# A scan layer's product with C moved one group back, and the next layer's weights loaded into dead tiles

## The chip, the core and the metric

The kernel runs on one core of a Trainium2 chip. The core has five engines that matter here, each with its own instruction stream in program order: PE (TensorE, matrix products), DVE (VectorE), ACT (ScalarE), POOL (GpSimd) and SP, which issues the transfers (DMA). [...] The metric is the device time of one execution in microseconds (us).

## What is computed

Two layers on an image tensor `x` of shape (4, 384, 64, 64), both with a residual and a group norm ahead of them. Layer 0 is a selective scan (Mamba) over the 4096 pixels of each image, with 768 channels and 16 states per channel. Layer 1 is attention over 7 x 7 windows with 12 heads.

```python
# layer 0, per image (L = 4096 tokens, 768 channels, 16 states)
xz = einsum('blc,dc->bld', layernorm(xs), in_proj_w); xb, z = split(xz, 2)
xc = silu(causal_conv4(xb) + conv_b)
dt, Bm, Cm = split(einsum('bld,ed->ble', xc, x_proj_w))      # 24, 16, 16
dt = softplus(einsum('blr,dr->bld', dt, dt_w) + dt_b)
h  = exp(dt * A) * h + (dt * xc) * B         # the recurrence, over tokens
y  = sum_n(h * C) + xc * D
x  = x + einsum('bld,cd->blc', y * silu(z), out_proj_w)
# layer 1
qkv = w_qkv @ group_norm(x) + b_qkv
logits = q . k in the 7 x 7 window (edge padding) + rel_bias
x  = x + w_proj @ (softmax(logits) @ v window) + b_proj
```

## The kernel before

Layer 0 goes through 64 steps (4 images of 16 chunks of T = 256 tokens). A step has 24 groups `m`: a group is 4 of the 16 states of one block of 128 channels (6 blocks d). Each group is two half-groups, so that a step has 48 slots. The lists in `AT` say in which slot the other work is issued; negative slots lie in the step before.

A group passes through four engines. ACT makes the decays exp(dt A) in PSUM (two instructions for each half). DVE or POOL makes the drive `db` = (dt x) B. DVE scans, two states at a time. POOL multiplies by C, in place. PE transposes and adds up over the states.

```python
def driven(I, m, h, eng):                                      # DVE or POOL
    db = w2.tile([P, NG, T], F32, tag="db", bufs=6)
    dtx = dtx_ps[:, d % 2, :] if eng is nc.vector else h["dtx"][d]
    eng.tensor_tensor(db[:, :, 1:], <dtx over 4 states>, h["B"][g][:, :, 1:], ALU.mult)

def decay(I, m, half, k, h):                                   # ACT
    act(da_ps[half][:, k, 1:], h["dt"]..., AF.Exp, scale=nega[:, d, n : n + 1])

def scans(I, m, half, hs):                                     # DVE
    nc.vector.tensor_tensor_scan(hs[:, pair, :], da_ps[half], dbs[I, m][:, pair, :],
                                 0.0, ALU.mult, ALU.add)

def kept_states(I, m, hs):                                     # ACT
    nc.scalar.copy(state[:, d, g * NG : (g + 1) * NG], hs[:, :, T - 1])

def with_c(I, m, h, hs):                                       # POOL, in place
    nc.gpsimd.tensor_tensor(hs, hs, h["C"][m % (NS // NG)], ALU.mult)

def summed(I, m, h, hs):                                       # PE
    for k in range(NG):
        for half in range(2):
            nc.tensor.matmul(y[:, d % 2, half, :], hs[:, k, half * P : (half + 1) * P],
                             ident, is_transpose=True, ...)
```

`dtx` (POOL) is dt times xc, and `dtx_ps` ACT's copy of it in PSUM for DVE. When a pair p of channel blocks has been added up, it is turned: ACT copies `yt` to `ys`, PE turns it back and adds xc D, DVE multiplies by the gate `sz` into `yg` (four buffers). The slots are those of `AT["turn"]`. The output projection then reads all three `yg`.

The loop over the groups:

```python
behind = []
for n in range(STEPS * M):
    hs = w2.tile([P, NG, T], F32, tag="hs", bufs=5)
    for half in range(2):
        others, acts = plan[I][2 * m + half]
        if half == 0 and behind:
            acts.insert(0, lambda last=behind[-1]: kept_states(*last[:2], last[3]))
        if 2 * n + half + 1 < len(halves):
            acts.insert(0, <decay of the next half, k = 0>)
            acts.insert(2, <decay of the next half, k = 1>)
        for what in acts: what()
        if half == 0:
            if behind: with_c(*behind[-1])
            ready = len(behind) - 1
            ...                              # held back once at the start of a pair
            for _ in range(ready): summed(*behind.pop(0))
        scans(I, m, half, hs)
        for what in others: what()
    behind.append((I, m, steps[I], hs))
```

So in group n ACT is given the state copy of group n-1, POOL the product of n-1, and PE the sum of n-2.

Layer 1 begins with its weights and its first stripe of x:

```python
w_qkv = wt.tile([P, NJ, 3 * C], F32); nc.sync.dma_start(w_qkv, qkv_wT...)   # 1728 KB
w_pj  = wt.tile([P, NJ, C], F32);     nc.sync.dma_start(w_pj, proj_wT...)   #  576 KB
for m in range(NJ):
    for j in range(NJ):
        nc.tensor.matmul(pvb[:, m : m + 1], w_pj[:, j, ...], qkb[:, ...], ...)
nc.vector.tensor_tensor(pjb, pjb, pvb[:, :NJ], ALU.add)
...
def projected(b, s, h, pool=ps, tag="mm"):
    xr = w2.tile(...); xn = w2.tile(..., bufs=1)
    nc.sync.dma_start(xr, x1s[b][...])
    for j in range(NJ): nc.vector.tensor_scalar(xn[:, j], xr[:, j], <mean>, <1/std>, ...)
    ...                                      # products with w_qkv for k, v and q
```

## Time and profile before

The median of three runs is 8284.29 us (8283.61 to 8287.84); the profiled execution took 8284.12 us, with a mean granted clock of TensorE of 0.963. What the profile gives for the instructions that the change touches:

| group | engine | times | busy, us | mean of one, ns |
|---|---|---|---|---|
| product with C, `hs<-hs,C` (L669) | POOL | 1536 | 3622.9 | 2363 |
| drive `db<-dtx,B` (L637) | POOL | 512 | 1207.6 | 2359 |
| drive `db<-dtx_ps,B` (L637) | DVE | 1024 | 1223.1 | 1200 |
| scan `hs<-da,db` (L656) | DVE | 3072 | 3623.3 | 1211 |
| decay `da<-dt,nega` (L96) | ACT | 6144 | 2898.3 | 474 |
| transposing sum `y<-ident,hs` (L682) | PE | 12288 | 1667.1 | 283 |

A line of a profile names the line of the kernel (L669), the engine, the operation, output and inputs with their shapes and how often it ran. "Busy" is the time in which instructions of that group ran. "Idle before" is how long the engine stood still just ahead of them, and the name after an arrow is the instruction whose end let it go on. The granted clock is the share of TensorE's full clock that it was given. The chain of work that ended last is followed back from the last instruction: at each step to what released it, or to the instruction before it on its engine.

### The profile page before, as it was taken

How to read it: one execution, taken by the hardware profiler on the slowest of the kernel's cores; microseconds unless marked ns; L12 is line 12 of the kernel's file. 1: busy time of each engine (PE TensorE's matmuls, PEld its weight loads, DVE VectorE, ACT ScalarE, POOL GpSimd, SP SyncE). 2: the span in 40 equal slices, each digit the busy share in tenths (PEclk: the TensorE clock that was granted, in tenths of full speed). 3: DMA queues.
4: the chain of work that ended last, by engine and by line, in shares of the span. 5: the costliest groups of instructions: out<-in, count | busy, mean ns of one | idle time of the engine just before them, and what ended most of it. 6: DMA issues, size and time to landing. Idle time of an engine off the chain costs nothing.

```text
span 8282.4 us, 144249 instructions
## 1 busy us (share of the span) xinstructions
PE 7499.3 (91%) x48570; PEld 5769.9 (70%) x48570; DVE 6666.8 (80%) x9783; ACT 6079.0 (73%) x17509; POOL 6954.3 (84%) x5223
## 2 busy tenths in 40 slices
PE   6898998899998989898989899899799999999999
PEld 5777777777777777777777777777555555555555
DVE  5888888888888888888888888888666666666666
ACT  4888888888888888888888888888555455455455
POOL 3999998989999898999989899999677777677777
PEclk9999999999999999999999999999799999999999
DMA  3212211221222122212211211121222233222322
GB/s 96 77 60 66 77 59 55 66 72 58 65 74 65 55 59 73 64 61 72 68 53 59 66 61 55 60 71 51 79 85 86 85 89 88 81 88 81 87 85 64
DMA packets 459624, 583.93 MB, mean 71 GB/s; under 512 B 195036, under 2 KB 343276, under 8 KB 458756
## 3 DMA queue, kind: packets, MB, share of 16 engines
q1 hardware_dynamic: 458884, 574.69, 22.7%
q8 instruction: 387, 6.34, 0.3%
q14 instruction: 353, 2.89, 0.1%
HBM read 472.02 MB, written 84.73 MB: 67 GB/s over the span
## 4 chain that ended last, share of the span: by engine, by line
PE 44%; ACT 21%; POOL 17%; DVE 12%; issue 5%; DMA 0%; SPq 0%; POOLq 0%; DVEq 0%; ACTq 0%
POOL hs L669 11%; ACT da L96 8%; DVE hs L656 6%; PE mm_ps L419 6%; PE y L682 5%; PE pt_ps L1047 4%; PE mm_ps L574 4%; PE mm_ps L426 3%; PE lg_ps L1016 3%; POOL db L637 3%; PE mm_ps L920 3%; PE mm_ps L1100 3%; PE mm_ps L953 3%; PE mm_ps L983 3%; PE pv_ps L1073 3%
## 5 line engine op out<-in xcount | busy, mean ns | idle before, releaser
L669 POOL TENSOR_TENSOR hs<-hs,C 128x1024 f32<-128x1024 f32 x1536 | 3622.9, 2363 | 478.4 <-ACT state L665 421.2
L656 DVE TENSOR_TENSOR_SCAN hs<-da,db 128x512 f32<-128x512 f32 x3072 | 3623.3, 1211 | 357.8 <-ACT da L96 210.2
L96 ACT ACTIVATE da<-dt,nega 128x255 f32<-128x255 f32 x6144 | 2898.3, 474 | 699.3 <-DVE hs L656 670.8
L1037 POOL TENSOR_SCALAR sg<-sg,rsum 128x308 f32<-128x308 f32 x1536 | 1621.4, 1076 | 638.9 <-DVE rsum L1035 637.2
L682 PE MATMUL y<-ident,hs 128*128 128x128 f32 x12288 | 1667.1, 283 | 468.1 <-POOL hs L669 450.5
L682 PEld LDWEIGHTS y<-ident,hs 128*128 128x128 f32 x12288 | 1443.1, 146 | 728.2 <-POOL hs L669 590.9
L637 DVE TENSOR_TENSOR db<-dtx_ps,B 128x1020 f32<-128x1020 f32 x1024 | 1223.1, 1200 | 110.9 <-ACT dtx_ps L609 105.7
L637 POOL TENSOR_TENSOR db<-dtx,B 128x1020 f32<-128x1020 f32 x512 | 1207.6, 2359 | 1.4 <-DMA B<-bcrows 1.4
L419 PE MATMUL mm_ps<-xn,w_in 128*128 128x256 f32 x4608 | 1160.5, 400 | 1.9 <-DVE xn L390 1.9
L96 ACT ACTIVATE sg<-sg,mx 128x308 f32<-128x308 f32 x1536 | 828.8, 541 | 250.8 <-DVE mx L1022 221.8
L419 PEld LDWEIGHTS mm_ps<-xn,w_in 128*128 128x128 f32 x4608 | 919.6, 206 | 132.3 <-DVE xn L390 2.6
L1022 DVE CUSTOM_DVE_ANT_0 sg<-lg_ps,bias 128x308 f32<-128x308 f32 x1536 | 643.2, 475 | 382.1 <-PE lg_ps L1016 382.1
L426 PE MATMUL mm_ps<-xb,dcv 128*128 128x256 f32 x3072 | 772.7, 400 | 9.4 <-DVE gm_b L270 9.4
L1065 ACT COPY tb<-pt_ps 88x512 f32<-88x512 f32 x384 | 222.3, 579 | 625.5 <-PE pt_ps L1061 625.4
L426 PEld LDWEIGHTS mm_ps<-xb,dcv 128*128 128x128 f32 x3072 | 592.0, 199 | 112.5 <-issue 19.9
L729 PE MATMUL mm_ps<-yg,w_out 128*128 128x256 f32 x2304 | 551.4, 380 | 0.0
L1052 DVE COPY ta<-pt_ps 110x512 f32<-110x512 f32 x768 | 492.7, 683 | 23.3 <-PE pt_ps L1047 23.3
L729 PEld LDWEIGHTS mm_ps<-yg,w_out 128*128 128x128 f32 x2304 | 434.3, 191 | 57.0
L1047 PE MATMUL pt_ps<-ident,sg 128*110 128x128 f32 x3072 | 417.6, 279 | 0.9 <-POOL sg L1037 0.8
L1047 PEld LDWEIGHTS pt_ps<-ident,sg 128*110 128x110 f32 x3072 | 322.8, 133 | 78.0 <-issue 48.4
L920 PE MATMUL mm_ps<-xn,w_qkv 128*128 128x512 f32 (+2 forms) x612 | 277.7, 592 | 60.4 <-DVE xn L907 53.2
L1016 PE MATMUL lg_ps<-k,q 32*128 32x308 f32 x3072 | 311.3, 473 | 0.0
(154 smaller groups left out, 10400.7 us busy)
## 6 DMA issues: line engine op xcount, KB each, us to landing
B<-bcrows SPq DMA_DIRECT2D x256, 512.0 KB
C<-bcrows SPq DMA_DIRECT2D x256, 512.0 KB
vw<-vd SPq DMA_DIRECT2D x1792, 33.0 KB
xr<-x SPq DMA_DIRECT2D x28, 1056.0 KB
vd<-v SPq DMA_DIRECT2D x280, 96.0 KB
xi<-in_x_dram SPq DMA_DIRECT2D x64, 384.0 KB
xo<-in_x_dram SPq DMA_DIRECT2D x64, 384.0 KB
x<-xo SPq DMA_DIRECT2D x64, 384.0 KB
```

Of the source, the lines that this page charges most:

```text
L96: ins = nc.scalar.activation(o, i, func, **kw)
L419: nc.tensor.matmul(pb[:, k, :], w_in[:, j, m * P : (m + 1) * P], xn[:, j, :], start=(j == 0), stop=(j == NJ - 1),)
L426: nc.tensor.matmul(pb[:, k, :], dcv[:, d, c, :], xb[:, d, c : c + T], start=(c == 0), stop=(c == KC - 1),)
L637: eng.tensor_tensor(db[:, :, 1:], dtx[:, 1:].unsqueeze(1).broadcast_to([P, NG, T - 1]), h["B"][g][:, :, 1:], ALU.mult,)
L656: nc.vector.tensor_tensor_scan(hs[:, pair, :].rearrange("p k t -> p (k t)"), da_ps[half].rearrange("p k t -> p (k t)"), dbs[I, m][:, pair, ...
L669: nc.gpsimd.tensor_tensor(hs, hs, h["C"][m % (NS // NG)], ALU.mult)
L682: nc.tensor.matmul(y[:, d % 2, half, :], hs[:, k, half * P : (half + 1) * P], ident, is_transpose=True, start=(first and half == 0 and d % ...
L729: nc.tensor.matmul(po, w_out[:, d, m * P : (m + 1) * P], h["yg"][d // 2][:, d % 2, :], start=False, stop=(d == ND - 1),)
L1016: nc.tensor.matmul(lg[:, :NK], blk["q"][pr, m, bl, :, :].rearrange("p r c -> p (r c)"), blk["k"][pr, m, :, bl * CB : bl * CB + CW], start= ...
L1022: nc.vector.tensor_tensor_reduce(sg[:, hh, :], lg[:, :NK], bias[:, 4 * m + hh, :], -1.0, BIG, ALU.add, ALU.min, mx[:, hh : hh + 1],)
L1037: nc.gpsimd.tensor_scalar(sg[:, hh, :], sg[:, hh, :], rs[:, hh : hh + 1], None, ALU.mult)
L1047: nc.tensor.transpose(pt[: KN[c], col : col + P], sg[:, 2 * pair + hh, KOFF[c] : KOFF[c] + KN[c]], ident,)
```

## The change

Three things are changed in layer 0. POOL's product with C is given one group later: in group n it is that of n-2, and PE's sum that of n-3. For that `hs` gets six buffers instead of five. The aim is that POOL finds the scans done and the state copy made when it comes to a product. The state copy itself goes ahead of both decays of its slot. To make room, `ys` has one buffer instead of two and `yg` three instead of four. The slots in `AT` are set anew for this order.

At the seam, `w_in`, `dcv` and the tile `xo` are moved to a pool that lives through both layers. In the last step, `w_in` and `dcv` are no longer read, and layer 1's weights and first input are loaded into them. The first input is normalised there as well. The product of the projection with the value bias, which needs `w_pj`, moves behind the first stripe's projections.

```diff
-             'x': ((-11, -11, -8, -7), (-11, -11, -7, -5), (-7, -6, -4, -3)),
-             'c': ((-3, -2, 0, 5), (3, 3, 7, 8), (15, 16, 18, 19)),
+             'x': ((-11, -11, -8, -7), (-11, -11, -9, -6), (-7, -6, -4, -3)),
+             'c': ((-5, -4, -2, 1), (3, 3, 7, 8), (15, 16, 18, 19)),
 ... norm two slots later, single slots of z, burst and softplus changed by one or two
-             'dtx': (-5, -3, 9, 13, 23, 29),
+             'dtx': (-5, -4, 7, 12, 22, 28),
 ... driven: group 11 from DVE to POOL, group 16 from POOL to DVE, three slots changed
-             'turn': (21, 24, 26),
+             'turn': (23, 25, 28),
-             'e0': (-4, -2, 11, 12, 23, 26),
-             'h0': (-4, -1, 11, 16, 24, 32),
+             'e0': (-4, -2, 11, 13, 23, 23),
+             'h0': (-4, -1, 11, 16, 24, 35),
 ... two entries of first
@@ turn
-                    h["ys", p] = w2.tile([P, 2, 2, P], F32, tag="ys", ...)
+                    h["ys", p] = w2.tile([P, 2, 2, P], F32, tag="ys", ..., bufs=1)
-                    yg = w2.tile([P, 2, T], F32, tag="yg", ..., bufs=4)
+                    yg = w2.tile([P, 2, T], F32, tag="yg", ..., bufs=3)
@@ loads in the last step
+            def early():
+                nc.sync.dma_start(w_qkv, qkv_wT.rearrange("(k p) m -> p k m", p=P))
+                nc.sync.dma_start(w_pj, proj_wT.rearrange("(k p) m -> p k m", p=P))
+                nc.sync.dma_start(x_first..., x1s[0][:, : n0 * HW]...)
+            def early_normed():
+                for j in range(NJ):
+                    nc.vector.tensor_scalar(x_first[:, j, :, :], x_first[:, j, :, :],
+                        gms1[0][:, j, 0:1], gms1[0][:, j, 1:2], ALU.subtract, ALU.mult)
+            slot_of(STEPS - 1)(24, early)
+            slot_of(STEPS)(AT["turn"][2] - 15, early_normed)
@@ the loop over the groups
-                hs = w2.tile([P, NG, T], F32, tag="hs", ..., bufs=5)
+                hs = w2.tile([P, NG, T], F32, tag="hs", ..., bufs=6)
-                    if half == 0 and behind:
-                        acts.insert(0, lambda last=behind[-1]: kept_states(*last[:2], last[3]))
                     if 2 * n + half + 1 < len(halves):
                         ...
+                    if half == 0 and behind:
+                        acts.insert(0, lambda last=behind[-1]: kept_states(*last[:2], last[3]))
                     if half == 0:
-                        if behind:
-                            with_c(*behind[-1])
-                        ready = len(behind) - 1
+                        if len(behind) > 1:
+                            with_c(*behind[-2])
+                        ready = len(behind) - 2
-            with_c(*behind[-1])
+            for what in behind[-2:]:
+                with_c(*what)
@@ layer 1
-            w_qkv = wt.tile(...); nc.sync.dma_start(w_qkv, ...)
-            w_pj = wt.tile(...); nc.sync.dma_start(w_pj, ...)
-            ... product of w_pj with the value bias, here ahead of everything
+            def values_bias(): ...     # the same product
-            ahead = projected(*todo[0], stripes[0], ps_l, "lg")
+            ahead = projected(*todo[0], stripes[0], ps_l, "lg", xn=x_first)
             ...
             vw = window(*todo[0], 0)
+            values_bias()
```

## Prediction

> **What bounds the kernel now.** I read the busy shares first, then busy time by stage, the waits inside the first layer, the chain that ended last, and the seam between the layers. The page opens with busy time and share of each engine:

> ```profile
> PE 7499.3 (91%) x48570; PEld 5769.9 (70%) x48570; DVE 6666.8 (80%) x9783; ACT 6079.0 (73%) x17509; POOL 6954.3 (84%) x5223
> ```

> That average mixes two layers. By stage (columns: stretch in us, length, then PE, weight load, DVE, ACT, POOL busy with counts, granted clock, DMA share, GB/s):

> ```profile
> 3000.00:4000.00 1000.00, 900.44 (x4989) 760.11 (x4989) 891.51 (x857) 847.83 (x2402) 913.68 (x616) 0.96 0.21 66
> 7000.00:8282.00 1282.00, 1221.04 (x10958) 723.94 (x10955) 825.63 (x2667) 642.18 (x1995) 921.21 (x903) 0.99 0.28 82
> ```

> The first row is the scan layer (it ends at about 5954 us), the second the attention layer. In the scan layer four engines lie between 85% and 91%, so none is simply the bound, and each is idle for a tenth. From 1000 to 5700 us the trace has 1239 products with C; at 24 a step that is 51.6 steps, so a step takes 4700/51.6 = 91.0 us and a slot (48 a step) 1.90 us. The waits in that stretch (engine, line, waited for: us, times, longest):

> ```profile
> POOL hs L669 <- ACT state L665: 350.2, 401, 5.2
> ...
> ACT da L96 <- DVE hs L656: 538.3, 669, 6.0
> ...
> PE y L682 <- POOL hs L669: 339.0, 239, 2.8
> ...
> DVE yg L712 <- PE mm_ps L705: 163.7, 98, 2.6
> DVE db L637 <- ACT dtx_ps L609: 82.3, 101, 1.1
> ```

> POOL's only large wait is 350.2/51.6 = 6.8 us a step, for ACT's small copy of the last states: the product overwrites `hs` in place, so it must wait until ACT has read the last column, and ACT reaches that copy only after whatever stands before it. Does it matter? One stretch of the chain that ended last, in order of time (start, us, what):

> ```profile
> 4089.42 0.13 ACT state L665
> 4089.55 0.07 issue
> 4089.61 1.83 POOL hs L669
> 4091.44 0.49 issue
> 4091.93 0.73 POOL dtx L603
> 4092.66 2.21 POOL hs L669
> 4094.86 0.07 issue
> 4094.93 2.35 POOL db L637
> 4097.28 2.31 POOL hs L669
> 4099.60 0.04 issue
> 4099.64 1.97 PE y L682 x8
> 4101.61 5.89 PE mm_ps L419 x24
> ```

> ACT had been on the chain since 4059, with its burst of Silu and two table loads in it. Then the chain crosses to POOL by this very wait, stays 10 us there, and 14 us on PE, up to the gate on DVE at 4114.06. Counted over 1000 to 5700 us, it goes from ACT's state copy to POOL's product 124 times, 2.4 times a step. It spends 29% of that stretch on ACT, 27% on PE, 24% on POOL, 14% on DVE. So this wait is on the path, though not alone.

> The seam, PE's instructions with the idle time before them:

> ```profile
> 5951.49 2.75 PE L729 MATMUL mm_ps<-yg,w_out 128*128 128x256 f32 x12
> 5964.45 3.97 PE L879 MATMUL pvb<-qkb,w_pj 128*128 128x1 f32 x18 [10.20 <-DMA w_pj<-in_proj_wT_dram]
> 5969.53 12.83 PE L920 MATMUL lg_ps<-xn,w_qkv 128*128 128x192 f32 x36 [1.11 <-DVE xn L907]
> ```

> PE ends layer 0 at 5954.24 and starts attention's first projection at 5969.53: 15.3 us between, for the weights, the product with the bias and the first input.

> [...] here the two engines' drive products take 2359 and 1200 ns. POOL's work therefore can't be shrunk or cheaply moved, only its waiting. [...]

> **The change part by part.** *Product one group later.* At group n POOL now multiplies group n-2, whose scans and state copy were done about a group (3.8 us) ago. The waits of 0.87 us on average (350.2/401), 5.2 at most, should vanish nearly all. No instruction goes or comes: POOL's work stays 82.6 us a step (90.75% of 91.0). Removing all 6.8 us would be the upper bound. What the path gets back is less. At each of 2.4 crossings POOL will have one product more behind it, at most 2.36 us, so at most 2.4 x 2.36 = 5.7 us a step. DVE (89%) and ACT (85%, saturated for 30 us around the burst) are close behind; I take half, a choice of mine: 2.8 us.

> *PE's transposes and the gate.* Each sum comes one group later, with six buffers instead of five, so a buffer's slack before its reuse is the same. The turn moves from slots (21, 24, 26) to (23, 25, 28): the gate gets three slots after the transposing back instead of two. That can return part of the 163.7/51.6 = 3.2 us a step that DVE waits there; but these waits hang on POOL through PE, so I count nothing beyond the half above.

> *The re-tuned slots.* `dtx` for the later blocks stands one or two slots earlier. The chain goes by dtx, dtx_ps and db 49 times, about once a step, and DVE waits 82.3/51.6 = 1.6 us a step there; I take 0.3. One drive product changes from DVE to POOL and one back: no net work.

> *The state copy before the decays.* It is now ahead of both decays of its slot instead of between them. From its start to the next instruction's is about 0.12 us on the chain. The chain crosses from DVE's scan to a decay 219 times (4.2 a step), half of them in such a slot: 2.1 x 0.12 = 0.25 us lost.

> Sum per step: 2.8 + 0.3 - 0.25 = 2.85 us; over 64 steps 182 us.

> *The seam.* The weights (1728 and 576 KB) and the first input go into `w_in` and `dcv` from slot 24 of the last step, when PE has used both for the last time (in the changed plan their last reader stands at slot 16 of the step before). 3.4 MB at the 327 GB/s which the seam shows is 10 us of DMA beside a step of 91. The 15.3 us shrink to about 1. The bias product, 3.97 us, moves behind the projection, where PE waits for DVE anyway (5.07 of 10 us busy from 6000 to 6010); I count 1 us. Gain 13 us. Attention's own steps keep their instructions; I expect no change there.

> Together 8284 - 182 - 13 = 8089, say 8085 us.

> **Rivals.** (1) *Another loop takes over.* DVE and ACT wait for one another (538.3 us of ACT), and ACT is full through the burst. If POOL's slack is used up by that loop, a step gains only about 1 us: 8284 - 64 - 13 = 8207. For it: four engines near 90%. Against: 124 crossings. (2) *The whole wait comes back*, 6.8 us a step, and POOL runs without a gap: 8284 - 435 - 13 = 7836. Against: PE is on the chain for 27%, its work has not shrunk, and ACT's 30 us are untouched. (3) *The new order hurts*: the copy ahead of the decays, the single `ys` and three `yg` make ACT or PE wait, say 1 us a step lost: 8335. `ys` is written 16 slots apart and read two slots later, and `yg` of slot 28 is last read by slot 24 of the next step, so four slots (7.6 us) remain; I see no new wait there. (4) *PE's clock*: granted 0.96 in the scan layer[...]. Each per cent of a 27% share is worth 0.25 us a step, 16 us in all.

> **Range and chances.** 2% is 166 us, which needs a step shorter by (166 - 13)/64 = 2.4 us; my 2.85 is little above, and the half is the weak term. A quarter instead of the half gives about 8180, three quarters about 8000. I take 7975 to 8215. Faster by over 2%: 0.57; within: 0.38; slower by over 2%: 0.05, because only rival 3 leads there, and it would have to take 2.6 us a step on top of the seam's gain.

> **What would show it.** Right: the wait of POOL's product for the state copy falls from 350 to under 50 us in the same stretch; POOL's share in the scan layer rises from 91% to 93 to 95%; a step takes about 88.2 us; the crossing from state copy to product leaves the chain; PE goes from the output projection to L920's counterpart within 2 us. Wrong: POOL's wait only changes its name (scan, drive product or C), or POOL's share stays at 91% while ACT's waits for scans grow; or the seam still shows a DMA ahead of the first projection.

## The result and the profile after

The changed kernel takes 7988.47 us (median of four runs, 7986.13 to 7990.36), the kernel before 8284.22 (median of four). The ratio is 0.9642, with a 95% interval of 0.9625 to 0.9659: 296 us or 3.6% faster. The prediction said 8085, with a range of 7975 to 8215.

The page of the changed kernel opens with these shares:

```profile
PE 7414.1 (93%) x48570; PEld 5584.4 (70%) x48570; DVE 6674.9 (84%) x9783; ACT 6024.9 (75%) x17509; POOL 6932.1 (87%) x5223
```

By stage, a thousand microseconds of the scan layer and one of attention (columns as before):

```profile
3000.00:4000.00 1000.00, 934.50 (x5261) 766.27 (x5261) 938.73 (x904) 884.46 (x2533) 962.29 (x664) 1.00 0.21 67
6000.00:7000.00 1000.00, 958.39 (x8523) 568.03 (x8516) 645.10 (x2086) 500.14 (x1556) 716.75 (x703) 0.99 0.29 86
```

In the scan layer POOL is now busy 96%, DVE 94%, where it had been 91% and 89%. The number behind it, the granted clock, went from 0.96 to 1.00; it turns out to matter. From 1000 to 5400 us the trace has 1220 products with C, so 50.8 steps, and a step takes 4400/50.8 = 86.6 us instead of 91.0. The waits of that stretch, by engine:

```profile
POOL hs L677 <- ACT state L673: 107.7, 110, 4.8
POOL dtx L611 <- ACT dt L588: 66.8, 54, 2.7
...
ACT state L673 <- DVE hs L664: 266.4, 315, 2.0
ACT da L96 <- DVE hs L664: 140.1, 255, 5.6
...
DVE hs L664 <- ACT da L96: 198.6, 372, 1.5
...
DVE hs L664 <- ACT db L637: 8.5, 51, 0.3
...
DVE db L645 <- ACT dtx_ps L617: 3.2, 3, 1.8
...
PE y L690 <- POOL hs L677: 129.1, 183, 1.4
```

POOL's wait for the state copy fell from 6.8 to 107.7/50.8 = 2.1 us a step. A new wait of 1.3 us, for dt, stands beside it. On DVE two waits are all but gone: `yg` (3.2 us a step) no longer stands in the list, and `dtx_ps` went from 1.6 to 0.1. ACT and DVE still wait for one another: ACT for scans 406 us (266.4 + 140.1; 505 in the kernel before in the same stretch), DVE for decays 199 us (158 before). PE's wait for POOL at the sums fell from 315 to 129 us. The seam on PE:

```profile
5671.38 2.75 PE L737 MATMUL mm_ps<-yg,w_out 128*128 128x256 f32 x12
5673.97 10.81 PE L949 MATMUL lg_ps<-dcv,w_in 128*128 128x192 f32 x36
...
5705.28 2.06 PE L905 MATMUL pvb<-qkb,w_in 128*128 128x1 f32 x18
```

Attention's first projection follows the output projection with no gap. Layer 0 ends at 5674 us instead of 5954, 280 us earlier; the rest of the span is 2310 us instead of 2328 (both from the two profiled executions).

### The profile page after: what moved, and what is told of

It is laid out like the page before. It is cut to its first block, busy times and chain, and to the rows that moved or that the text cites. A ratio compares the mean times of both kernels' runs of the same rounds, so it can differ in the third digit from the quotient of the medians.

```text
span 7984.4 us, 143739 instructions
## 1 busy us (share of the span) xinstructions
PE 7414.1 (93%) x48570; PEld 5584.4 (70%) x48570; DVE 6674.9 (84%) x9783; ACT 6024.9 (75%) x17509; POOL 6932.1 (87%) x5223
## 3 DMA queue, kind: packets, MB, share of 16 engines
q14 instruction: 348, 2.85, 0.1%
## 5 line engine op out<-in xcount | busy, mean ns | idle before, releaser
L664 DVE TENSOR_TENSOR_SCAN hs<-da,db 128x512 f32<-128x512 f32 x3072 | 3664.1, 1213 | 370.5 <-ACT da L96 249.3
L96 ACT ACTIVATE da<-dt,nega 128x255 f32<-128x255 f32 x6144 | 2864.1, 472 | 192.8 <-DVE hs L664 179.3
L690 PE MATMUL y<-ident,hs 128*128 128x128 f32 x12288 | 1606.6, 277 | 225.4 <-POOL hs L677 184.6
L690 PEld LDWEIGHTS y<-ident,hs 128*128 128x128 f32 x12288 | 1384.6, 142 | 508.6 <-POOL hs L677 330.0
L427 PE MATMUL mm_ps<-xn,w_in 128*128 128x256 f32 x4608 | 1101.5, 385 | 59.3 <-ACT sz L96 37.7
L96 ACT ACTIVATE sg<-sg,mx 128x308 f32<-128x308 f32 x1536 | 828.8, 541 | 252.1 <-DVE mx L1051 236.1
L427 PEld LDWEIGHTS mm_ps<-xn,w_in 128*128 128x128 f32 x4608 | 840.6, 191 | 215.6 <-ACT sz L96 63.0
L434 PE MATMUL mm_ps<-xb,dcv 128*128 128x256 f32 x3072 | 722.3, 381 | 0.0
L434 PEld LDWEIGHTS mm_ps<-xb,dcv 128*128 128x128 f32 x3072 | 566.3, 189 | 93.1 <-issue 20.9
L673 ACT COPY state<-hs 128x4 f32<-128x4 f32 x1535 | 298.9, 195 | 357.9 <-DVE hs L664 337.6
L611 POOL TENSOR_TENSOR dtx<-dt,xc 128x256 f32<-128x256 f32 x384 | 280.6, 731 | 109.4 <-ACT dt L588 109.4
```

The source lines that it names most:

```text
L96: ins = nc.scalar.activation(o, i, func, **kw)
L427: nc.tensor.matmul(pb[:, k, :], w_in[:, j, m * P : (m + 1) * P], xn[:, j, :], start=(j == 0), stop=(j == NJ - 1),)
L434: nc.tensor.matmul(pb[:, k, :], dcv[:, d, c, :], xb[:, d, c : c + T], start=(c == 0), stop=(c == KC - 1),)
L664: nc.vector.tensor_tensor_scan(hs[:, pair, :].rearrange("p k t -> p (k t)"), da_ps[half].rearrange("p k t -> p (k t)"), dbs[I, m][:, pair, ...
```

## The experiments

Twelve kernels were run, all timed against the kernel before (8283.1 to 8285.3 us in these groups). "Low clock" is counted from the windows view: of the 1100 stretches of 4 us between 1000 and 5400 us, those with a mean granted clock under 0.9. "Against changed" is the difference of two medians that were taken in different groups.

| kernel | median, us | against before | against changed | low clock |
|---|---|---|---|---|
| before | 8284 | | +296 | 11.8% |
| changed | 7988 | -296 | | 0.7% |
| `defer_only` | 8147 | -137 | | 7.5% |
| `retune_only` | 8187 | -97 | | 4.5% |
| `seam_only` | 8268 | -15 | | 11.9% |
| `pe_filler` | 8191 | -92 | | 4.3% |
| `filler_busy` | 8386 | +101 | | 9.1% |
| `after_oldslots` | 8230 | -54 | +242 | 13.2% |
| `after_oldturn` | 8103 | | +115 | 1.4% |
| `kept_between` | 8021 | | +33 | 1.5% |
| `kept_first_together` | 8067 | | +79 | 1.0% |
| `other_first` | 8008 | | +20 | 2.7% |
| `one_drive_dve` | 8057 | | +68 | 1.1% |
| `one_drive_pool` | 7978 | | -10 | 0.8% |

### One part at a time

`defer_only`: the kernel before, with this alone.

```diff
-                hs = w2.tile(..., bufs=5)
+                hs = w2.tile(..., bufs=6)          # ys 2 -> 1, yg 4 -> 3
-                            with_c(*behind[-1])
-                        ready = len(behind) - 1
+                            with_c(*behind[-2])     # if len(behind) > 1
+                        ready = len(behind) - 2
```

> The kernel before with the deferral alone: product with C one group later, six hs, one ys, three yg; slots, seam and the place of the state copy (between the decays) as before. Theory D (the deferral carries the gain, since POOL's wait for the state copy stood on the path): 8284 - 64 x 3.6 = about 8055 us, POOL's wait for the state copy under 150 us of 1000 to 5400. Rival S (the new slots carry it: what went is DVE's waiting for yg, dtx_ps and db): 8200 us or more, DVE's waits for yg and dtx_ps still above 3 us a step together.

Measured: 8147.04 us, ratio 0.9835 (0.9819 to 0.9852), 60% of what theory D expected of the deferral, more than rival S allowed it. POOL's waits from 1000 to 5400 us, in the kernel before:

```profile
POOL hs L669 <- ACT state L665: 330.1, 376, 5.2
POOL hs L669 <- DVE db L637: 32.6, 48, 0.7
```

and with the deferral alone:

```profile
POOL hs L669 <- ACT state L665: 129.9, 208, 5.2
POOL dtx L603 <- ACT dt L580: 92.2, 84, 3.8
POOL e L624 <- ACT e L96: 41.7, 52, 3.2
POOL dtx L603 <- DVE hs L656: 24.0, 14, 1.9
```

The wait for the state copy falls by 200 us, but POOL, now running ahead, meets the next things that ACT has not made yet: dt for its `dtx`, and `e`. In sum it still waits 288 us instead of 363. Behind dt stands a wait of PE that the kernel before hardly has: dt is summed on PE from three parts, and PE waits 131.2 us (2.0 before) for the one that DVE makes, `spe`. In the changed lists DVE's part of the first softplus stands two slots earlier, and in the changed kernel this wait is 14.6 us; no run moves that slot alone. DVE's waits for `yg` and `dtx_ps` fall as well, from 151.7 to 101.7 and from 76.2 to 26.2 us.

`retune_only`: the new `AT` lists in the kernel before, except the turn, which the old loop does not allow in its new place.

```diff
-             'dtx': (-5, -3, 9, 13, 23, 29),
+             'dtx': (-5, -4, 7, 12, 22, 28),
 ... all other lists of AT as changed, but 'turn': (21, 24, 26)
```

> The kernel before with the new slots alone, the turn excepted, which keeps (21, 24, 26); loop, buffers and seam as before. Theory D: 8284 within 40 us, POOL still waits some 6 us a step for the state copy. Rival S: 8180 us or less.

Measured: 8186.71 us, ratio 0.9883 (0.9868 to 0.9898), 7 us above what rival S expected. POOL still waits 305.4 us for the state copy, so the 97 us came without that wait's going. What went is DVE's waiting for `yg` (151.7 to 43.9 us) and for `dtx_ps` (76.2 to 6.6):

```profile
DVE hs L656 <- ACT db L629: 153.1, 138, 2.0
DVE yg L712 <- PE mm_ps L705: 43.9, 59, 1.2
DVE hs L656 <- issue: 27.9, 91, 0.4
DVE db L637 <- ACT dtx_ps L609: 6.6, 13, 0.5
```

In exchange DVE's wait for ACT's first column of `db` grew, from 75.1 to 153.1 us. Neither theory wins: the two parts have each a share. How much of either share came through PE's clock is taken up below.

`seam_only`: the changed kernel with loop, `AT` and buffers of the kernel before, so that only the early loads remain.

```diff
 # against the kernel before
+            slot_of(STEPS - 1)(24, early)
+            slot_of(STEPS)(AT["turn"][2] - 13, early_normed)
```

> The kernel before with the seam alone (weights and first input into dead tiles); loop, slots and buffers as before. Prediction's estimate: 13 us gained, 8271. By the traces of before and after (the end of layer 0 to the end: 2328.2 and 2310.4 us): 18 us gained, 8266. Rival: attention's own steps also go another way with the new placement, and 30 us or more are gained.

Measured: 8267.93 us, ratio 0.9981 (0.9974 to 0.9988): 15 us, between the two estimates and without the rival's further gain.

`after_oldslots`: the changed kernel with the old lists, turn included.

```diff
-            AT = {...}      # new
+            AT = {...}      # the kernel before's
```

> The changed kernel with all the slots of the kernel before (turn too); deferral, copy ahead of the decays and seam kept. Theory D: at most 60 us slower than 7988, about 8045. Rival S: 8150 us or more.

Measured: 8230.15 us, 242 us slower than the changed kernel: rival S, and far beyond what `retune_only` makes of the slots. It is even slower than `defer_only`, though it has the seam as well. Between these two only the seam and the place of the state copy differ; taking the seam at its 15 us, the copy ahead of the decays costs 8230 - 8147 + 15 = 98 us with the old slots, by difference. With the new ones it is the reverse, as the next runs show. PE's wait for `spe` is at its largest here, 200.7 us; POOL waits 164.0 us for dt and 98.9 for `e`, and the low clock has 13.2% of the stretch. So part of the 242 us may be that clock.

`after_oldturn`: one list of them.

```diff
-             'turn': (23, 25, 28),
+             'turn': (21, 24, 26),
```

> The changed kernel with the turn back in slots (21, 24, 26), all other slots new. If the gate's three slots are what took DVE's 3.2 us of waiting for yg away: these waits come back to 1 to 3 us a step, and 50 to 150 us are lost: 8040 to 8140. If they went because the sums come in time by the deferral and the other slots: within 25 us of 7988.

Measured: 8103.11 us, 115 us lost, in the first range but not for its reason. DVE waits only 10.0 us for `yg` in the whole stretch. ACT's waits now hold a line, the last, that the changed kernel's list does not have:

```profile
ACT state L673 <- DVE hs L664: 327.5, 353, 2.1
ACT da L96 <- DVE hs L664: 120.7, 198, 5.7
ACT xc L96 <- PE mm_ps L434: 77.1, 50, 3.0
ACT ys L701 <- PE y L690: 53.3, 90, 2.0
```

ACT comes to the copy `ys` before PE has finished the sum, which the deferral has made one group later, and the decays stand behind it. The same wait is there in the other two runs with the deferral and the old turn (33.4 us in `defer_only`, 58.8 in `after_oldslots`) and not in the kernel before or in `retune_only`. POOL's wait for the state copy grows too, from 107.7 to 164.8 us; that both follow from ACT's waiting for `ys` is argued, not shown.

### The state copy and the decays

`kept_between`: the copy between the decays again.

```diff
-  # [copy, decay 0, other work, decay 1, ...]
+  # [decay 0, copy, decay 1, other work, ...]
```

> The changed kernel with the state copy back between the two decays, nothing else. By the prediction's estimate of 0.25 us a step lost by the copy ahead of the decays: 16 us faster than the changed kernel, 7972. Rival: with the copy first, POOL's product is freed earlier and the decays wait for the same scan anyway: equal or up to 20 us slower than 7988.

Measured: 8021.46 us, 33 us slower. The 0.25 us a step of the prediction had the wrong sign. `kept_first_together` parts the copy from what stands between the decays.

```diff
-                        acts.insert(2, <decay 1>)
+                        acts.insert(2 - (half == 0), <decay 1>)
   # [copy, decay 0, decay 1, other work, ...]
```

> The changed kernel with the state copy still ahead, but the two decays of that slot next to one another (the other ACT work of the slot behind them instead of between). If the copy's being first is what gains 33 us over the place between the decays: equal to 7988 within 10 us, or faster. If the gain lies in the other work standing between the decays, with slots tuned for that: about 8020.

Measured: 8067.39 us, 79 us slower. So it is not the copy's being first that gains (8067 with it first, 8021 with it between, the decays next to one another in both); it is the other work standing ahead of the second decay. Where it stands behind, it comes later: POOL's wait for dt grows from 66.8 to 97.8 us and DVE's for `dtx_ps` from 3.2 to 20.7. `other_first` puts that work ahead of everything.

```diff
+                    if half == 0 and len(acts) > 3:
+                        acts.insert(0, acts.pop(2))
   # [other work, copy, decay 0, decay 1, ...]
```

> The changed kernel, but in the slots with a state copy the first piece of other ACT work stands ahead of copy and decays instead of between the decays, so that ACT does it while it would wait for the scan (406 us of such waits in 4400). If that wait is idle time to be filled: 20 to 60 us faster, 7930 to 7970. If the slots are tuned for the decays apart: 30 to 100 us slower, as with the decays together (8067).

Measured: 8008.25 us, 20 us slower, under the 30 to 100 of the second guess; the ratio to before, 0.9666 (0.9652 to 0.9680), just overlaps that of the changed kernel (0.9625 to 0.9659). ACT's waits for scans do shrink, from 406 to 283 us (150.2 + 132.9), but no gain comes of it: POOL's wait for the state copy grows from 107.7 to 138.9 us and DVE's for the first column of `db` from 8.5 to 30.2.

### PE's clock

In the kernel before, once a step PE stands still for 2.8 us until POOL has multiplied group 15. This is one such place, first PE's instructions, then windows of 2 us (PE, weight load, DVE, ACT, POOL, then the granted clock):

```profile
4004.77 1.09 PE L682 MATMUL y<-ident,hs 128*128 128x128 f32 x8
4008.64 1.97 PE L682 MATMUL y<-ident,hs 128*128 128x128 f32 x8 [2.78 <-POOL hs L669]
4010.41 7.21 PE L419 MATMUL mm_ps<-xn,w_in 128*128 128x256 f32 x24
```

```profile
4005.00:4007.00 2.00, 0.86 (x8) 0.63 (x6) 2.00 (x3) 1.68 (x5) 2.00 (x2) 1.00 0.28 98
4007.00:4009.00 2.00, 0.36 (x2) 0.36 (x3) 2.00 (x2) 0.96 (x4) 2.00 (x3) 0.59 0.31 2
4009.00:4011.00 2.00, 2.00 (x10) 1.91 (x9) 2.00 (x3) 1.97 (x7) 1.92 (x4) 0.50 0.25 2
4011.00:4013.00 2.00, 2.00 (x7) 1.55 (x6) 2.00 (x3) 1.97 (x6) 2.00 (x2) 0.50 0.24 49
4013.00:4015.00 2.00, 2.00 (x8) 1.68 (x7) 2.00 (x3) 1.75 (x5) 2.00 (x2) 0.71 0.59 213
4015.00:4017.00 2.00, 2.00 (x11) 1.77 (x10) 2.00 (x3) 1.86 (x6) 2.00 (x2) 1.00 0.00 0
```

The clock falls within the gap and is at half for some 6.8 us, from about 4007.3 to 4014.2. The eight transposes take 1.97 us, which elsewhere take about 1.09, and the projection 7.21. It is so step after step, with two lengths: in 51 steps the transposes there have a median of 1.97 us, and the projection takes by turns about 7.2 us, when the low clock lasts 6.8 us, and 6.1, when it lasts 3.4. Just these instructions stand on the chain that the prediction printed. `pe_filler` tests whether the low clock itself costs anything: useless products are put into the gap, and nothing is taken away.

```diff
+            def filler():                 # read by nothing
+                f = bank()
+                for k in range(5):
+                    nc.tensor.matmul(f[:, 0, :], ones_c, dsd[:, 0:2, :]..., ...)
+            for I in range(1, STEPS - 1):
+                slot_of(I)(33, filler)
```

> The kernel before with five products of constants (128x256, not read by anything) for PE in slot 33 of each step, just where PE stands 2.8 us still waiting for POOL; nothing else. Clock theory (each such gap is followed by some 4 us at about half the granted clock, on the path): the low clock goes from 12% of the layer to under 5%, and the time falls by 1 to 2 us a step, to 8150 to 8220. Rival (the low clock costs nothing, as the path runs elsewhere): 8284 within 15 us. Third: the added work itself delays the sums: 8300 or more.

Measured: 8190.92 us, ratio 0.9887 (0.9872 to 0.9901). With more work than before, the kernel is 92 us faster. The same place in its trace:

```profile
4030.07 1.09 PE L682 MATMUL y<-ident,hs 128*128 128x128 f32 x8
4031.00 2.32 PE L805 MATMUL mm_ps<-dsd,ones_c 128*128 128x256 f32 x10
4033.94 1.09 PE L682 MATMUL y<-ident,hs 128*128 128x128 f32 x8 [0.62 <-POOL hs L669]
4034.87 5.35 PE L419 MATMUL mm_ps<-xn,w_in 128*128 128x256 f32 x24
```

The gap is 0.62 us, the transposes take 1.09 and the projection 5.35, in nearly every step within 0.01 of that. With a projection of 6.65 us as the mean of 7.2 and 6.1, that is 0.88 + 1.30 = 2.2 us of PE less a step, of which 92/62 = 1.5 us reach the end (the products stand in 62 of the 64 steps). Other waits shrink with it, though their slots stand as before: DVE's for `yg` from 151.7 to 87.9 us, POOL's for the state copy from 330.1 to 259.5. The control puts the same five products one half-group later, behind the gap.

```diff
-                slot_of(I)(33, filler)
+                slot_of(I)(35, filler)
```

> Control for the filler in the gap: the kernel before with the same five products, one half-group later (slot 35), behind the sum for which PE waits, so that the gap of 2.8 us stays. Clock theory: the low clock stays near 12% and nothing is gained; the 1.9 us of products stand on the path: 8284 to 8400. Rival (the filler helped by shifting the PSUM banks, not by the clock): 8190 again, as with the filler in the gap.

Measured: 8386.20 us, ratio 1.0123 (1.0108 to 1.0138). The gap stays, and the products run in the slow spell:

```profile
4078.78 1.44 PE L682 MATMUL y<-ident,hs 128*128 128x128 f32 x8 [2.76 <-POOL hs L669]
4080.00 3.71 PE L805 MATMUL mm_ps<-dsd,ones_c 128*128 128x256 f32 x10
4083.55 5.34 PE L419 MATMUL mm_ps<-xn,w_in 128*128 128x256 f32 x24
```

The low clock did not stay quite at 12% (9.1%), but the same work in two places, the rotation of PSUM banks nearly the same, differs by 195 us. The loss fits PE's own time there: from the first transpose to the end of the projection it takes 10.3 us in the mean instead of 8.4, and 1.9 x 62 = 118 us is near the 101 measured. A gain by the banks is not needed, and the rival is out as the main cause: the gap was to be filled, and its filling is worth more than the work costs. The changed kernel fills it with its own work, at the same place of a step:

```profile
3137.56 1.09 PE L690 MATMUL y<-ident,hs 128*128 128x128 f32 x8 [1.36 <-POOL hs L677]
3138.85 5.42 PE L427 MATMUL mm_ps<-xn,w_in 128*128 128x256 f32 x24 [0.20 <-DVE xn L398]
```

The gap is 1.36 us, and in 49 of 51 steps the projection takes about 5.4 us.

The parts alone shorten the same stretch of PE: from the first transpose to the end of the projection it is 8.4 us in the mean before, 7.0 with `defer_only`, 6.8 with `retune_only` (where the gap there has a median of 1.4 us) and 6.9 in the changed kernel. That is 1.5 and 1.7 us a step, or 93 and 106 us of PE, beside gains of 137 and 97 us. So PE's clock is a rival to the waits named for both parts, and no run parts the two.

### What bounds it now

`one_drive_dve` moves a drive from POOL to DVE, `one_drive_pool` another one the other way.

```diff
 # one_drive_dve: group 11
-   (15, 0)
+   (15, 1)
 # one_drive_pool: group 22
-   (36, 1)
+   (36, 0)
```

> The changed kernel with the drive of group 11 on DVE instead of POOL: POOL 2.36 us a step less, DVE 1.20 more. If POOL (95% busy) is now the bound: 1 to 2 us a step gained, 7860 to 7925. If POOL and DVE (93%) bound together: within 30 us of 7988. If DVE's loop with ACT is the bound: 1.2 x 64 = 77 us slower, about 8065.

Measured: 8056.71 us, 68 us slower, 1.06 us a step for 1.20 us of work: what is added to DVE costs nearly its whole length, while the 2.36 us taken from POOL become waiting (for the state copy 270.1 us instead of 107.7).

> The changed kernel with one more drive on POOL (group 22 from DVE to POOL): DVE 1.20 us a step less, POOL 2.36 more (to 85.0 of 86.6 us). If DVE's loop alone is the bound now (a drive more on DVE cost 68 us): 30 to 70 us faster, about 7940. If POOL's throughput binds as well: 30 to 100 us slower, about 8050.

Measured: 7978.05 us, ratio to before 0.9630 (0.9616 to 0.9645) against 0.9642 (0.9625 to 0.9659) of the changed kernel: 10 us less, which these intervals do not tell apart. POOL takes the 2.36 us and is then busy 98%:

```profile
1000.00:5400.00 4400.00, 4065.66 (x23059) 3390.52 (x23058) 4073.11 (x3878) 3883.59 (x11095) 4327.48 (x2920) 1.00 0.21 67
```

So POOL's 96% were no bound of their own, but with 98% there is hardly more to shift: DVE begins to wait for POOL's `dtx` and drives (24.2 and 13.5 us). The result fits neither guess. Together the two runs say that DVE, in its loop with ACT, bounds the layer, with POOL just behind; that relief on DVE alone would pay was not tried.

## Why the prediction was right or wrong

*The wait on the path*: right. The crossing from state copy to POOL was where time could be had, and the deferral alone took 137 us, 2.1 us a step. Of the upper bound of 5.7 us the prediction took half, 2.8, which was somewhat large. It gave DVE and ACT close behind as the reason, and did not foresee that POOL would meet dt and `e` next; its own sign of being wrong, a wait that changes its name, came in part in `defer_only` (158 us of new waits for 233 that went). That POOL's work could be neither shrunk nor cheaply moved was the author's estimate: no run shrank it, and one drive moved to DVE, tried in the changed kernel alone, cost 68 us. Nor did it see that the deferral also shortens PE's gap, and so may gain by the clock. "The waits ... should vanish nearly all" failed: 107.7 us are left of 330 in the same stretch, the longest 4.8, not under 50.

*The re-tuned slots*: the direction right, the size wrong. "I take 0.3" was the worst-sized term of the sum: alone the slots are worth 97/64 = 1.5 us a step, and under the deferral with the copy first (`after_oldslots`) 242/64 = 3.8. The prediction counted only the drive's `dtx_ps`. It set the `yg` waits aside as hanging on POOL; `retune_only` takes 108 us of them away while POOL waits on for the state copy. And it had no term for PE's clock at group 15's sum, which `retune_only` keeps up in 36 of 49 steps.

*The state copy ahead of the decays*: wrong. It counted 0.12 us for the copy and overlooked that the second decay moves behind the next piece of ACT's other work. With the new slots the two together gain 33 us instead of losing 16 (the copy's being first costs 46, the other work between the decays gains 79); with the old ones they cost about 98. The place in the list and the slots had been set for one another.

*The seam*: right, 15 us measured, 13 predicted. The bias product took 2.06 us behind the projections.

*Sum*: 137 + 97 + 33 + 15 = 282 of 296 us. That the parts nearly add up is in part chance, since the slots alone lack the turn, the copy's effect changes sign with the slots, and the deferral and the slots both shorten the same slow stretch of PE. That the time fell within the stated range, near its lower end, is in part luck too: the deferral was put 42 us too high (179), the slots 78 too low (19), the copy 49 too low (-16). One reading in the prediction is slightly off and enters no sum: POOL's work is 83.0 us a step (4282.5/51.6), not 82.6.

*Rivals.* The first (another loop takes over, 1 us a step) did not take over so early; it is the bound now, after 4.4 us a step. The second, the whole wait, came nearer than I gave it room for, though not through POOL alone. The third has its grain in `after_oldslots`. The fourth, PE's clock as a loss, was the wrong way round: with PE busy for 934.50 us from 3000 to 4000 us instead of 900.44, the granted clock was 1.00 instead of 0.96.

*The signs.* POOL's share was to be 93 to 95% and is 95 to 96, a step 88.2 us and is 86.6, the seam under 2 us and is without a gap. That the crossing leaves the chain could not be read: in the changed kernel the profile follows the chain back only to the seam.

*What stays open.* How much of the 296 us is the clock. In the kernel before, filling one gap a step is worth 92 us net of the filler's own work, nearly as much as all new slots alone. The low clock goes from 11.8% to 0.7% in the changed kernel, but no run holds the clock low while the rest is changed. At the place above PE has regained some 2.1 us a step (1.97 to 1.09 and 6.65 to 5.42), of which more or less may have reached the end.

## What to carry to other kernels

Where an engine waits for a small copy that another engine makes late in its order, taking the dependent work one round later costs one buffer and may free it (137 us here); but look at once at what that engine will ask for next (here dt, `e` and, behind dt, DVE's `spe`), and try those producers earlier in the same change. Try a new order and the slots around it together: with the old slots the same order lost 242 of 296 us. And look at the granted clock behind PE's short gaps when they recur on the path: here even useless products paid in the gap (92 us gained), and not behind it (101 us lost).

## What the runs showed of the hardware that was not expected

In windows of 1 us between 1000 and 5400 us the kernel before has 76 spells at half the full clock, 48 of about 3.4 us and 28 of about 6.8, and all 76 begin on one grid of 3.413 us, within 0.07 us. PE was not idle all the time ahead of a fall: in the 3.41 us ahead of the fall at 4007.34 it was busy for 1.94 us, and ahead of that at 4099.50 for 0.79. Nor did every spell follow a gap of 2.8 us: in the changed kernel the clock fell at 1576.90 with no longer gap than 1.55 us near it and PE busy for 1.38 of the 3.41 us before. How much idle time lowers the clock is not shown.
